# A load stage written as one pinned list of pieces, with a narrower first transform and the weight replicas on another queue

## The chip, the core and the metric

The kernel runs on one core of a Trainium2 chip: TensorE (PE, with its weight loads shown as PEld), VectorE (DVE), ScalarE (ACT), GpSimd (POOL) and SyncE (SP), which share the core's DMA engines. The metric is the device time of one execution in microseconds (us); smaller is better.

## The reference

Two blocks follow each other on x, 4 batches of 32 images (tokens) of 128x128, float32. The first block is what this change touches:

```python
x = x + _L0_conv_ref(_ln_c(x), ...)      # spectral attention over the 32 tokens, then two spectral mixers
t = t + _L0_ffn_ref(_ln_t(t), ...)       # recurrent layer along the rows
x = x + _L1_conv_ref(_ln_c(x), ...)      # 2x up, leaky ReLU, 2x down with given 12x12 filters
t = t + _L1_ffn_ref(_ln_t(t), ...)
```

`_ln_c` normalises every row of 128 values. In `_L0_conv_ref` each token is normalised as an image; keys, queries and values come from a few low frequencies of its Fourier transform times learnt weights, plus a skip; a softmax over 32x32 token pairs per head mixes the values; the result is projected, added to the tokens, and goes through two mixers that again multiply low frequencies. The kernel uses that most of this is linear: it needs of each image only its low-frequency spectrum and the products of images with each other (a Gram matrix), and mixes whole images by one 128x128 matrix (CTbd).

## The kernel before, in words

**Load stage (up to the first channel mix).** XA holds all images with the row index h on the partitions. SP loads them in 16 DMAs of 512 KB (`load`), with constants and small weights between them. Work is in eight half batches k of 16 images. For each: `stats` takes the row statistics on DVE and their inverse root (ACT's Sqrt and a Newton step on DVE); `normalise` scales each image in place, on ACT or DVE by the image's number; `transform` multiplies each image (as the 128x128 stationary operand) with a table of 130 columns (L862): 64 for the low-frequency spectrum and 66 for a real basis of the Gram product. ACT copies three images at a time out of PSUM (L863). A second transform gives the spectrum (ps_pf, L870) and the Gram operand (ps_pr, L874, copied to Rn by L879). Then SP writes the normalised half batch to DRAM (`normed`, L881).

Per batch, `scores` turns the spectrum: ACT copies it from PSUM (L888) and DVE transposes 32x32 blocks (L889). It is spread to all heads (ps_fr, Frep), multiplied on DVE with replicated key/query weights (L909, L923, L924) and brought by PE transposes to the scores psc. `gram` forms the image products pg. `attend` is the softmax and ends in a block of CTbd (L1020). `weights` prepares the learnt weights: Mx (key/query) and Dx (value/projection) go to DRAM and come back replicated to all partitions (`everywhere`, five DMAs each on SP, tiles md and dd, into Mrep and Drep); the first mixer's weights go through DRAM as m1d, transposed, and come back to every partition (L723, L724). `filters` checks that the given filters are of rank one and makes their taps (tile hankel).

After the last normed write SP reloads all images in the other layout, channels on the partitions (L1071, XR, eight DMAs of 1 MB). Each waits for the writes of `normed` and for the readers of XA.

**After it.** The next stage interleaves the channel mix (pm, L1092, with CTbd and XR) with weighted spectra: 32 DVE products `df` (L1286, from Drep and Frep, a ring of eight) and sums on PE (ps_y, L1299, eight steps of four). Then norms, the token-mixing stage (230 to 410 us in the profile), the recurrence, the convolutions and the second recurrence.

**What sets the order.** Inside `with in_order():` each instruction of PE, DVE, ACT and POOL is chained to the one before it on its engine, so the order of the program text is kept. In the load stage the text is generated by Python generators stepped in turns (`step`), and the middle part is outside any `in_order`, so the framework's scheduler places it. The later stages are strings of piece names (SUMS, NORMS, MIXERS, CONVOLUTIONS), walked in order. SP is not chained.

Of the kernel before, what the change touches and what calls it, by code (L numbers as in the profile page):

```python
# [32 lines left out]
P = 128  # L33
NB, NT = 4, 32
NH = 16
# [119 lines left out]
    IRI0.2 M4b.1 de.1 M4c.1 FHG.1 gBc.1 g3.2 Z0.2 FS2.0 Z1.2 g2.2 QG0.1 FS1.0 FS0.0 g1.2 g0.2 ST2.2 A2.2 sq2.2 FS3.0  # L155
    IRS0.1 TA1.1 ZS2.2 AF.0 sq3.2 ST0.2 QG1.1 PW.0 ZS3.2 ZD.2 A0.2 TA0.1 PF.2 sq0.2 R1a.1 sq1.2 LD2.1 FZ.2 SQ.2
    R0b.1 R0a.1 FHIa.3 R1b.1 AO.0 IRS2.1 M1.2 TA2.1 LD0.2 FHIb.3 R2b.1 XN1a.0 XN0b.0 PS.2 M2.2 TA3.1 QI0.3 XN0a.0
    PG1.2 XN1b.0 QI1.3 R2a.1 PG2.2 XT0.0 M2b.2 IRI2.3 R3a.1 R3b.1 XC0.0 XT1.0 P2.2 IRI0.3 Z2.3 M3.2 Z3.3 WX0.0 XC1.0
    P3.2 XN2a.0 al.2 Z0.3 M4a.2 g2.3 M4b.2 g3.3 Z1.3 g0.3 de.2 GB.2 M4c.2 BN0.0 g1.3 FS2.1 FS1.1 ZS2.3 ST2.3 sq1.3
    sq2.3 FHG.2 ST0.3 QG0.2 XN3b.0 IRS0.2 A2.3 A0.3 TA1.2 gBc.2 TA0.2 XN2b.0 FS3.1 PF.3 sq0.3 FS0.1 WC0.0 XT2.0  # L160
    ZS3.3 QG1.2 sq3.3 WX1.0 FZ.3 ZD.3 R1b.2 AF.1 R0b.2 IRS2.2 SQ.3 TA3.2 XC2.0 PW.1 R0a.2 PG1.3 R1a.2 M1.3 BN1.0
    LD2.2 PS.3 TA2.2 R3a.2 XN3a.0 WC1.0 M2.3 AO.1 WX2.0 R2a.2 FHIa.4 BN2.0 R3b.2 PG2.3 XN0b.1 FHIb.4 M2b.3 XT3.0
    P2.3 XN0a.1 M3.3 WC2.0 al.3 QI0.4 R2b.2 QI1.4 P3.3 XC3.0 IRI0.4 XN1a.1 XT0.1 Z1.4 M4a.3 IRI2.4 WX3.0 XN1b.1 Z0.4
    XC0.1 g1.4 M4b.3 de.3 g0.4 M4c.3 Z3.4 Z2.4 GB.3 FHG.3 BN3.0 FS3.2 g3.4 FS1.2 FS2.2 LD0.3 QG0.3 ST0.4 g2.4 FS0.2
    gBc.3 A0.4 QG1.3 ZS3.4 ZS2.4 IRS0.3 sq1.4 TA1.3 sq2.4 ST2.4 LD2.3 R1a.3 TA0.3 A2.4 WC3.0 PF.4 R1b.3 XN2b.1 FZ.4
    AF.2 ZD.4 XT1.1 sq3.4 R0b.3 WX0.1 IRS2.3 PW.2 R0a.3 SQ.4 sq0.4 PG1.4 TA2.3 XC1.1 M1.4 PS.4 BN0.1 TA3.3 AO.2 M2.4
    M2b.4 R2b.3 XN3a.1 XN2a.1 WC0.1 XT2.1 FHIa.5 R3b.3 LD0.4 R3a.3 XC2.1 P2.4 XN3b.1 XN0b.2 M3.4 PG2.4 XN0a.2 P3.4
    FHIb.5 QI0.5 QI1.5 XT3.1 WX1.1 IRI0.5 al.4 R2a.3 XN1a.2 XC3.1 BN1.1 M4a.4 Z1.5 IRI2.5 de.4 WC1.1 M4b.4 M4c.4
    XN1b.2 FS0.3 GB.4 gBc.4 WX2.1 XT0.2 BN2.1 g1.5 XN2b.2 Z3.5 WC2.1 FHG.4 FS3.3 XC0.2 QG0.4 WX3.1 FS1.3 FS2.3 QG1.4
    LD2.4 XT1.2 XN2a.2 XN3a.2 IRS0.4 XC1.2 TA1.4 BN3.1 Z2.5 TA0.4 AF.3 g2.5 Z0.5 R1b.4 XT2.2 IRS2.4 g0.5 WC3.1  # L170
    FHIa.6 sq0.5 R1a.4 R0a.4 R0b.4 WX0.2 ZS2.5 PW.3 g3.5 ZS3.5 BN0.2 TA2.4 AO.3 FHIb.6 ZD.5 ST2.5 sq2.5 FS0.4 R2b.4
    XN3b.2 ST0.5 XC2.2 sq1.5 R2a.4 sq3.5 WC0.2 A0.5 TA3.4 WX1.2 R3b.4 BN1.2 A2.5 PF.5 QI0.6 IRI0.6 XN0a.3 R3a.4
    XN0b.3 XT3.2 Z0.6 WC1.2 FZ.5 SQ.5 M1.5 QI1.6 PG1.5 XC3.2 g0.6 Z1.6 IRI2.6 PS.5 Z2.6 M2.5 g1.6 WX2.2 Z3.6 g2.6
    g3.6 P2.5 BN2.2 M2b.5 M3.5 XN1a.3 XT0.3 FS2.4 PG2.5 P3.5 FS3.4 XC0.3 ST0.6 al.5 M4a.5 WC2.2 A0.6 ST2.6 de.5
    M4b.5 M4c.5 WX0.3 A2.6 BN0.3 XN1b.3 PF.6 ZS2.6 sq0.6 ZS3.6 sq3.6 FS1.4 GB.5 FZ.6 FHG.5 WC0.3 SQ.6 QG0.5 WX3.2
    sq2.6 AF.4 IRS0.5 TA0.5 PW.4 PG1.6 sq1.6 gBc.5 XT1.3 QG1.5 M1.6 XC1.3 LD0.5 ZD.6 BN3.2 TA1.5 R0a.5 XN2a.3 R0b.5
    PS.6 LD2.5 AO.4 IRS2.5 M2.6 XN3b.3 XN2b.3 TA3.5 WC3.2 XT2.3 P2.6 M2b.6 XN3a.3 WX1.3 XC2.3 R1a.5 PG2.6 XT3.3
    TA2.5 R1b.5 FHIa.7 FHIb.7 XN0a.4 R3a.5 BN1.3 M3.6 R2a.5 XN0b.4 XC3.3 WC1.3 WX2.3 XN1b.4 QI0.7 R2b.5 XT0.4 P3.6
    QI1.7 R3b.5 al.6 BN2.3 M4a.6 de.6 XN1a.4 IRI0.7 IRI2.7 XN2b.4 XC0.4 WC2.3 Z1.7 LD0.6 M4b.6 WX3.3 g1.7 XT1.4
    M4c.6 BN3.3 FHG.6 XC1.4 WC3.3 WX0.4 Z0.7 Z2.7 FS2.5 g0.7 FS0.5 g2.7 GB.6 Z3.7 FS1.5 QG0.6 ST0.7 g3.7 BN0.4  # L180
    IRS0.6 FS3.5 A0.7 sq0.7 ZS2.7 TA1.6 ST2.7 gBc.6 ZS3.7 XN2a.4 ZD.7 WC0.4 QG1.6 A2.7 TA0.6 XT2.4 PF.7 R1b.6 sq1.7
    R1a.6 sq3.7 LD2.6 WX1.4 AF.5 FZ.7 R0a.6 SQ.7 XN3b.4 IRS2.6 PW.5 R0b.6 PG1.7 sq2.7 TA2.6 M1.7 LD0.7 XC2.4 PS.7
    AO.5 XN0a.5 XN3a.4 BN1.4 WC1.4 XN0b.5 R2a.6 M2.7 R2b.6 TA3.6 XT3.4 XN1a.5 XC3.4 WX2.4 R3b.6 M2b.7 P2.7 PG2.7
    XN1b.5 BN2.4 WC2.4 XT0.5 M3.7 WX3.4 R3a.6 al.7 P3.7 BN3.4 M4a.7 de.7 XC0.5 LD2.7 FS2.6 M4b.7 XT1.5 XN2b.5 XC1.5
    GB.7 WC3.4 M4c.7 FS3.6 XN2a.5 gBc.7 WX1.5 BN1.5 WC1.5 FS0.6 XT2.5 FHG.7 WX0.5 QG0.7 FS1.6 XN3b.5 AF.6 BN0.5
    IRS0.7 WC0.5 TA0.7 R0a.7 QG1.7 XC2.5 TA1.7 PW.6 XN3a.5 TBL.7 WX2.5 XT3.5 IRS2.7 R1a.7 AO.6 BN2.5 XN0b.6 TA2.7
    XC3.5 XN0a.6 R0b.7 WC2.5 R1b.7 XN1b.6 XT0.6 XN1a.6 XC0.6 FS1.7 FS0.7 WX3.5 AF0.7 XT1.6 BN3.5 TA3.7 XN2b.6 R2a.7
    R2b.7 XN3b.6 WC3.5 WX0.6 XN2a.6 XC1.6 XN3a.6 XT2.6 WX1.6 XC2.6 BN0.6 PW0.7 XT3.6 FS2.7 AO0.7 WC0.6 R3b.7 R3a.7
    WX2.6 BN1.6 XN02a.7 XN00a.7 FS3.7 XN00b.7 XC3.6 XN02b.7 WC1.6 WX3.6 XT02.7 XT00.7 XC02.7 XC00.7 AF2.7 WX02.7
    BN2.6 BN3.6 WC2.6 WC3.6 PW2.7 AO2.7 XN20b.7 WX00.7 XN22b.7 XN20a.7 XN22a.7 XT20.7 BN02.7 BN00.7 XC20.7 XT22.7  # L190
    XC22.7 WX20.7 BN20.7 WC00.7 WC02.7 WX22.7 BN22.7 WC20.7 WC22.7
# [15 lines left out]
C_E = 0  # L207

C_DW = C_E + 130
C_CR = C_DW + 96  # L210
C_SW = C_CR + 128
C_EH2 = C_SW + 256
# [10 lines left out]
C_N = C_DB + NB  # L223
# [8 lines left out]
def _constants():  # L232
    c = np.zeros((P, C_N), np.float64)
# [14 lines left out]
    basis = np.concatenate([(h2[:, None] % 2 == np.arange(2)) / np.sqrt(32), np.cos(turn) / np.sqrt(32),  # L248
                            np.sin(turn) / np.sqrt(32)], 1)
    c[:, C_E + 64 : C_E + 128] = rows.real.T @ basis  # L250
    c[:, C_E + 128 : C_E + 130] = (rows.imag.T @ basis)[:, :2]
# [3 lines left out]
    c[:, C_CR : C_CR + 64] = cols.real  # L255
    c[:, C_CR + 64 : C_CR + 128] = -cols.imag
# [10 lines left out]
    for b in range(NB):  # L267
        o = 32 * b
        c[o : o + KW, C_SW : C_SW + 128] = sw.real
        c[o : o + KW, C_SW + 128 : C_SW + 256] = sw.imag  # L270
        c[o, C_DCB + o : C_DCB + o + 32] = 1.0


        c[o + 1 : o + 9, C_CL : C_CL + 16] = 128.0
        c[o, C_CL : C_CL + 8] = 128.0

        c[o, C_SIG] = -1.0
        c[o : o + 32, C_DB + b] = 1.0
        c[o, C_DCM] = 1.0
        c[o : o + 32, C_ID : C_ID + 32] = np.eye(32)  # L280
        c[o : o + 32, C_BO + o : C_BO + o + 32] = 1.0
        c[o : o + KW, C_TP] = twice[:, 0]
    return np.ascontiguousarray(c.astype(np.float32))
# [3 lines left out]
def _network(  # L287
# [94 lines left out]
    def row_stats(st, n, mean, var):  # L382

        d = sm([P, NG], "rw_d")[:, :n]
        tt(mean, st[:, :, 1], st[:, :, 4], ALU.add)
        ts(mean, mean, 0.5, None, ALU.mult)
        tt(d, st[:, :, 1], st[:, :, 4], ALU.subtract)
        stt(d, d, 0.25, d, ALU.mult, ALU.mult)
        tt(var, st[:, :, 2], st[:, :, 5], ALU.add)
        stt(var, var, 1.0 / P, d, ALU.mult, ALU.add)  # L390
# [170 lines left out]
    ndcm = aw.tile([P, 1], F32, name="ndcm")  # L561
# [28 lines left out]
    nc.sync.dma_start(cst[:, :C_SW], consts[:, :C_SW])  # L590

    for v in range(4):
        nc.gpsimd.dma_start(skips[:, v : v + 1], scal[v * NH : v * NH + NH].unsqueeze(0).broadcast_to([8, NH]))
    load(0, 2 * TC)
    load(0, 3 * TC)
    taps_in = []
    if redo is not None:
        for k in range(2):
            F = wp.tile([2 * PAD + 1, 2, 12], F32, name=f"F{k}")
            taps_in.append(F)  # L600
            for j in range(2):
                f = up[j, 0] if k == 0 else dn[j]
                nc.gpsimd.dma_start(F[:, j, :], f[P // 2 - PAD : P // 2 + PAD + 1, :, P // 2])
    nc.sync.dma_start(cst[:, C_SW:], consts[:, C_SW:])
    for b in range(1, NB - 1):
        for t0 in range(0, NT, TC):
            load(b, t0)
    nc.gpsimd.memset(CTbd, 0.0)
    nc.gpsimd.tensor_copy(rep4, cst[:, C_ID : C_ID + 32].unsqueeze(1).broadcast_to([P, 4, 32]))

    dram = early.enter_context(tc.tile_pool(name="replicas", bufs=1, space=bass.MemoryType.DRAM))

    def weights():

        mw_, mp_ = skips[:, 2:3], skips[:, 3:4]

        def hermitian(wr, wi, d, dm):

            tt(d, wr[:, 31:0:-1], wr[:, 1:], ALU.subtract)
            ts(d, d, dm, 0.5, ALU.mult, ALU.mult)
            tt(wr[:, 1:], wr[:, 1:], d, ALU.add)
            tt(d, wi[:, 31:0:-1], wi[:, 1:], ALU.add)
            ts(d, d, dm, -0.5, ALU.mult, ALU.mult)
# [1791 lines left out]
```

## Time and profile before

| | |
|---|---|
| three runs | 869.56, 870.73, 875.28 us; median 870.73 |
| profiled execution | 870.38 us, span 868.6 us |
| mean granted PE clock | 0.939 |
| busy over the span | PE 750.8, DVE 710.9, ACT 649.4, POOL 361.2 us |
| DMA | 83.22 MB; HBM read 47.46 MB, written 33.66 MB |
| first statistics / first normalisation | 6.38 / 17.67 us |
| last normed write issued / first reload issued | 106.4 / 111.6 us |
| first channel mix / first ps_y | 136.83 / 141.60 us |

A group's row gives line, engine, operation, output and inputs, shape and count, then busy time and mean duration. A row of the timeline gives start and length of a run of equal instructions, and in brackets the idle time before it and what ended it. A stage's row gives its length and each engine's busy time with the count of instructions, the granted PE clock, the mean busy share of the DMA engines, and GB/s.

### The profile page before, as it was taken

The page shows a single profiled execution, that of the slowest core. Times are in us where ns is not written, and L with a number is a line of the kernel's source. Part 1 is how long each engine was busy: PE and PEld are TensorE (multiplying, and loading weights), DVE is VectorE, ACT ScalarE, POOL GpSimd, SP SyncE. Part 2 cuts the span into 40 slices and gives each one's busy share as a digit, 9 for nine tenths or more (in the row PEclk, how much of TensorE's full clock was granted, in tenths as well). Part 3 has the DMA queues.
Part 4 walks back from the last instruction along what each step waited for, and adds up shares of the span by engine and source line. Part 5 has one row for each costly group of instructions (what it writes and reads, how often), then busy time and mean ns, then how long its engine had stood idle before and what let it go on. Part 6 is the DMA issues. An engine that isn't in the chain of part 4 may idle for free.

```text
span 868.6 us, 31057 instructions
## 1 busy us (share of the span) xinstructions
PE 750.8 (86%) x12550; PEld 560.5 (65%) x12550; DVE 710.9 (82%) x2330; ACT 649.4 (75%) x1669; POOL 361.2 (42%) x604
## 2 busy tenths in 40 slices
PE   1799967977878999899779979999999999998994
PEld 1566633336645555645349968888788877875994
DVE  3789668976598899899889978977878877677996
ACT  2588934585738689989779977887777887776994
POOL 2000000011435444365310016788788786961263
PEclk9799967996789899999999969999999999999998
DMA  9954992349611011120000000111111111118454
GB/s 224 260 153 94 250 366 103 137 204 276 162 51 49 26 49 35 42 73 25 25 1 1 1 3 17 40 41 40 28 41 28 41 28 40 40 40 291 172 186 148
DMA packets 105130, 83.22 MB, mean 96 GB/s; under 512 B 5457, under 2 KB 98129, under 8 KB 102865
## 3 DMA queue, kind: packets, MB, share of 16 engines
q1 hardware_dynamic: 104641, 80.86, 31.2%
q8 instruction: 101, 1.65, 0.8%
q0 software_dynamic: 288, 0.01, 0.2%
q14 instruction: 52, 0.43, 0.2%
q10 hardware_dynamic: 48, 0.26, 0.1%
HBM read 47.46 MB, written 33.66 MB: 93 GB/s over the span
## 4 chain that ended last, share of the span: by engine, by line
PE 44%; DVE 25%; ACT 14%; POOL 9%; issue 5%; DMA 1%; SPq 1%; DVEq 0%; ACTq 0%; POOLq 0%
PE ps_k L2068 5%; PE ps_scan L1915 4%; DVE XA L1587 4%; PE ps_d L2198 4%; ACT WXY L1917 4%; DVE XA L1586 4%; PE ps_st L862 3%; ACT yw L1917 3%; POOL XN L2047 3%; PE pm L1092 3%; PE ps_st L1429 3%; PE ps_r L2068 2%; PE ps_e L2205 2%; PE ps_y L1299 2%; POOL xn L2047 2%
## 5 line engine op out<-in xcount | busy, mean ns | idle before, releaser
L2188 DVE SCALAR_TENSOR_TENSOR U<-raw 128x512 f32<-128x512 f32 x128 | 89.8, 731 | 27.8 <-ACT raw L2180 27.6
L1916 DVE SCALAR_TENSOR_TENSOR ps_scan<-WXY,bs,ps_scan 128x128 f32<-128x128 f32 x376 | 105.5, 352 | 1.8 <-PE ps_scan L1915 0.8
L2068 PE MATMUL ps_k<-WXY,q 64*64 64x134 f32 x2048 | 86.0, 282 | 0.9 <-ACT WXY L2152 0.3
L2180 ACT COPY raw<-ps_k 128x512 f32<-128x512 f32 x128 | 71.0, 597 | 17.0 <-PE ps_k L2068 14.6
L2198 PEld LDWEIGHTS ps_d<-WXY,U 128*64 128x64 f32 x2048 | 66.7, 137 | 19.5 <-issue 12.1
L2047 POOL TENSOR_SCALAR XN<-XA,c_r,c_o 128x128 f32<-128x128 f32 x120 | 74.7, 631 | 5.0 <-issue 2.2
L2047 POOL TENSOR_SCALAR xn<-XA,f_r,f_o 128x128 f32<-128x128 f32 x120 | 67.2, 569 | 18.1 <-PE ps_x L2068 12.1
L2198 PE MATMUL ps_d<-WXY,U 128*64 128x67 f32 x2048 | 73.4, 224 | 1.2 <-ACT q L2211 0.9
L2068 PEld LDWEIGHTS ps_k<-WXY,q 64*64 64x64 f32 x2048 | 60.7, 135 | 6.4 <-DVE U L2188 0.8
L862 PE MATMUL ps_st<-cst,XA 128*128 128x130 f32 x256 | 42.8, 313 | 24.9 <-ACT XA L845 22.1
L2068 PE MATMUL ps_r<-WXY,XN 64*64 64x134 f32 x1024 | 59.0, 290 | 2.8 <-DVE XN L2047 1.3
L862 PEld LDWEIGHTS ps_st<-cst,XA 128*128 128x128 f32 x256 | 35.9, 212 | 29.1 <-ACT XA L845 23.1
L1644 ACT ACTIVATE xn<-XA,f_o,f_r 128x128 f32<-128x128 f32 x120 | 51.0, 489 | 4.6 <-DVE f_o L1626 3.4
L1423 ACT ACTIVATE Z<-Z,k,aB 128x128 f32<-128x128 f32 x128 | 51.0, 480 | 4.2 <-DVE Z L1418 4.0
L1586 DVE SCALAR_TENSOR_TENSOR XA<-ps_inv,r1B,xin 128x128 f32<-128x128 f32 x128 | 44.1, 345 | 8.1 <-PE ps_inv L1579 8.1
L1587 DVE SCALAR_TENSOR_TENSOR XA<-Z,gB,XA 128x128 f32<-128x128 f32 x128 | 46.3, 362 | 5.0
L2166 ACT COPY q<-ps_r 128x512 f32<-128x512 f32 x64 | 38.2, 597 | 13.2 <-PE ps_r L2068 12.8
L2027 POOL TENSOR_TENSOR c_r<-c_e,neg_half 128x16 f32<-128x16 f32 (+2 forms) x10 | 25.6, 2563 | 53.3 <-DVE c_e L2020 53.1
L506 PE MATMUL ps_inv<-invq,cst 64*128 64x512 f32 x128 | 41.4, 674 | 3.9 <-ACT invq L497 3.2
L456 PE MATMUL ps_wx<-xt,wvt 128*128 128x512 f32 x64 | 35.9, 643 | 6.7 <-ACT WXY L463 5.5
L845 ACT ACTIVATE XA<-XA,p_n,p_r 128x128 f32<-128x128 f32 x80 | 35.4, 491 | 7.6 <-DVE p_n L829 7.6
L2205 PE MATMUL ps_e<-WXY,q 128*64 128x67 f32 x1024 | 40.8, 222 | 0.0
(441 smaller groups left out, 2100.8 us busy)
## 6 DMA issues: line engine op xcount, KB each, us to landing
XA<-in_x_dram SPq DMA_DIRECT2D x16, 512.0 KB, 7.2
normed<-XA SPq DMA_DIRECT2D x8, 1024.0 KB, 6.1
XA<-normed SPq DMA_DIRECT2D x8, 1024.0 KB, 10.4
mixed<-XA SPq DMA_DIRECT2D x8, 1024.0 KB, 3.8
XA<-mixed SPq DMA_DIRECT2D x32, 256.0 KB, 5.3
xin<-in_x_dram SPq DMA_DIRECT2D x32, 256.0 KB, 3.3
turned<-XA SPq DMA_DIRECT2D x32, 256.0 KB, 2.5
out_dram<-res SPq DMA_DIRECT2D x52, 128.0 KB, 2.1
```

The source lines that it names most:

```text
L862: mm(p[:, i, :], XA[:, b, t0 + j + i, :], cst[:, C_E : C_E + 130], start=True, stop=True)
L1423: nc.scalar.activation(z, z, AF.Gelu, bias=k1, scale=aB[:, j : j + 1])
L1586: stt(a, p2[c, b][:, i], r1B[:, j : j + 1], xin[c, b - b % 2][:, b % 2, i], ALU.mult, ALU.add)
L1587: stt(a, Z[c][:, b, i], gB[c][:, n : n + 1], a, ALU.mult, ALU.add)
L1916: stt(p4, WX[:, :, h, :], s[:, 0:1], p4, ALU.mult, ALU.add)
L1917: nc.scalar.activation(dst, p4, AF.Sigmoid, bias=s[:, 1:2])
L2047: e.tensor_scalar(dst, src_, r, o, ALU.mult, ALU.add)
L2068: m = mm(dst, data, taps, start=(n == 0 and (i, j) not in last), stop=(n == 1), skip_group_check=True)
L2180: nc.scalar.copy(raw[u, k], banks["k", u][:, k])
L2188: stt(U[u][:, k].rearrange("p k s m -> p (k s m)"), v, SLOPE, v, ALU.mult, ALU.max)
L2198: mm(p[HALVES[s], m, b, REACH[k]], U[v][:, b, k, s, HALVES[m]], DR[:, k, REACH[k]], start=(m == 0 and b == 0 and k == 0), stop=(k == 1), s ...
L2205: mm(p[HALVES[j], b * P : b * P + P][:, REACH[m]], q3[v - 1][:, m, b, HALVES[j]], DC[:, m, REACH[m]], start=(b == 0 and m == 0), stop=(m = ...
```

## The change

1. **The load stage becomes a list.** LOADING is a string of some 600 pieces (S statistics, VA/VQ/VB/VC their factors, N and Nv normalisation on ACT or DVE, T, A, F, R, C the transforms and their copies, W the normed write, E to p the scores, G, g, H the Gram product, a, x, P, n, c the softmax, s scales, w weights). It is walked inside one `in_order` that also chains SP. The eight reloads of XR follow in the same block. Statistics are grouped as half batches 0, 1, 2+3, 4+5, 6+7; 90 images are normalised on ACT and 38 on DVE (80 and 48 before).
2. **First transform to 65 columns.** One real basis of 65 columns serves both the spectrum and the Gram operand; signs and scales move into second-transform tables. ACT or DVE copies seven, six and three images at a time.
3. **The spectrum is turned from PSUM**: the DVE transpose reads ps_pf with a stride; ACT's copy goes.
4. **Replicas by GpSimd's queue.** `everywhere` and the loads of value weights, vectors, mixer weights, ffn weights and filter taps, and the zeroing of hankel, are issued by POOL. Image loads, normed writes, m1d with its read-back, and the reloads stay on SP. All 16 image loads are issued before anything else of SP but the tables and constants.
5. **Weight symmetrisation** takes two ACT scalings and two DVE operations in place of six DVE operations. The scalar `ndcm` becomes a constant column.
6. **The filter check leaves the load stage**: it runs as nine pieces FL in MIXERS (token mixing).

```diff
+    first[:, C_F : C_F + 64] = rows.real.T @ basis
+    first[:, C_F + 64] = rows.imag.T @ basis[:, 0] / np.sqrt(2)
...
-    nc.sync.dma_start(cst[:, :C_SW], consts[:, :C_SW])
+    nc.sync.dma_start(tables, consts[:, C_N:])
...
+    for b in range(1, NB):
+        for t0 in range(0, NT, TC):
+            load(b, t0)
+        if b == 1:
+            nc.sync.dma_start(cst, consts[:, :C_N])
...
+    def T(k, i):
+        b, t0 = tokens(k)
+        j, n = next((j, i0) for j, (i0, i1) in enumerate(IMAGES) if i < i1)
+        if i == n:
+            held["st1", k, j] = psa.tile([P, 7, 65], F32, tag="st1", name="ps_st1")
+        mm(held["st1", k, j][:, i - n, :], XA[:, b, t0 + i, :], tables[:, C_F : C_F + 65], start=True, stop=True)
...
+    def W_(k, i):
+        b, t0 = tokens(k)
+        nc.sync.dma_start(normed[HB * k : HB * k + HB].rearrange("n h w -> h n w"), XA[:, b, t0 : t0 + HB, :])
+
+    def E_(b, i):
+        held["F4", b] = sp.tile([P, 16, NT], F32, tag="F4", name="F4")
+        nc.vector.transpose(held["F4", b].rearrange("p k w -> p (k w)"), held.pop(("pf", b)).rearrange("p t k -> p k t"))
...
+    def everywhere(t, dst, name):
+        n = t.shape[1]
+        d = dram.tile([NH, 8, n], F32, name=name)
+        nc.gpsimd.dma_start(d.rearrange("h k n -> k h n"), t)
+        for h in range(4):
+            nc.gpsimd.dma_start(dst[32 * h : 32 * h + 32],
+                                d[h::4].rearrange("g k n -> g (k n)").unsqueeze(0).broadcast_to([32, 4, 8 * n]))
+
+    def hermitian(w, d):
+        for r in range(2):
+            nc.scalar.mul(d[:, r], w[r][:, 31:0:-1], half_dc[: d.shape[0]])
+
+    def hermitian_sum(w, d):
+        for r in range(2):
+            stt(w[r][:, 1:], w[r][:, 1:], rest_dc[: d.shape[0]], d[:, r], ALU.mult, (ALU.add, ALU.subtract)[r])
...
+        elif k == 4:
+            everywhere(Mx.rearrange("p a w -> p (a w)"), Mrep.rearrange("p g k r m -> p g (k r m)"), "md")
+            nc.gpsimd.dma_start(Wv.rearrange("p w r k -> p (w r k)"), spec[:, W_VA:W_M1])
+            nc.gpsimd.dma_start(sc, scal.partition_broadcast(P))
...
+        elif k == 9:
+            held["mirv"] = big("ps_mirv")
+            mirrors(held["mirv"], Wv[:, 1], 4)
...
+        elif k == 13:
+            everywhere(Dx.rearrange("p a w -> p (a w)"), Drep.rearrange("p g k r j w -> p g (k r j w)"), "dd")
...
+        elif k == 16:
+            d = dram.tile([2 * KH, KW], F32, name="m1d")
+            nc.sync.dma_start(d.rearrange("k w -> w k"), m12[:KW, 0].rearrange("p r k -> p (r k)"))
+            nc.sync.dma_start(m1T.rearrange("p r k w -> p (r k w)"),
+                                d.rearrange("k w -> (k w)").unsqueeze(0).broadcast_to([P, KW * 2 * KH]))
...
+    with in_order(mybir.EngineType.SP):
+        for piece in LOADING.split():
+            name = piece.rstrip("0123456789.")
+            k, _, i = piece[len(name) :].partition(".")
+            loading[name](int(k), int(i or 0))
+        for h in range(0, P, ROWS):
+            nc.sync.dma_start(XR[:, h : h + ROWS, :], normed[:, h : h + ROWS, :])
+    early.close()
...
+        filtering = filters(m1, lambda name: psf.tile([P, 512], F32, tag="t", name=name))
+
+        def FL(c, k):
+            next(filtering)
```

The end of the list, from the last normalisation (N7.10) on:

```diff
+    T7.7 q2 qc2 a1.3 a1.4 T7.8 T7.9 T7.13 T7.11 N7.10 K2.5 T7.12 C5 T7.15 T7.14 T7.10 F6 A7.1 A7.2 W4 t2.0 F7 w14.0
+    t2.2 x1 w14.1 w15.0 tc2.0 tc2.2 t2.1 tc2.1 E3 r3.0 w13 rc3.0 r3.2 r3.3 rc3.3 a1.5 a1.6 a1.7 r3.1 rv3.2 W5 P1 G2
+    W6 a1.8 rc3.1 FK3 K3.0 K3.1 K3.2 g2 R6 H2 C6 W7 n0 a2.0 R7 C7 K3.3 p2 a2.1 q3 qc3 G3 g3 K3.4 w16 a2.2 K3.5 t3.0
+    H3 a2.3 a2.4 tc3.0 x2 w15.1 t3.2 t3.1 a2.5 a2.6 tc3.2 a2.7 P2 w17 a3.0 a2.8 tc3.1 p3 a3.1 a3.2 c1 a1.9 a3.3 a3.4
+    x3 c0 a3.5 a3.6 a3.7 P3 a0.9 a3.8 n3 n2 c2 a2.9 c3 a3.9 n1
```

## The prediction, before the changed kernel was run

> **What bounds it now.** I read the stages first, cut where the first channel mix starts (136.8 us) and where the token-mixing stage begins.
>
> ```profile
> core 0: us, PE busy (x) PEld busy (x) DVE busy (x) ACT busy (x) POOL busy (x), PEclk, DMA share, GB/s
> 0.00:20.00 20.00, 1.78 (x8) 1.79 (x9) 6.92 (x38) 3.22 (x7) 6.27 (x18) 1.00 0.95 219
> 20.00:110.00 90.00, 77.20 (x810) 56.93 (x810) 71.93 (x323) 71.07 (x177) 0.68 (x3) 0.94 0.79 193
> 110.00:136.80 26.80, 14.93 (x170) 8.71 (x162) 16.69 (x72) 6.94 (x16) 1.46 (x2) 0.63 0.81 325
> ...
> 230.00:410.00 180.00, 158.36 (x1615) 96.28 (x1615) 159.86 (x561) 140.71 (x389) 84.10 (x200) 0.95 0.15 42
> ```
>
> Up to 136.8 us DVE works 6.92 + 71.93 + 16.69 = 95.5 us, PE 93.9, ACT 81.2. No engine fills the stage: DVE idles 41 us. The last 27 us are a tail in which PE's clock falls to 0.63. The chain of waits shows what the tail is: one dependent sequence, with little beside it.
>
> ```profile
> 121.53 1.43 DVE KM L909 x2
> ...
> 129.57 0.20 DVE sums L772
> ...
> 136.83 4.84 PE pm L1092 x6
> 141.67 2.11 PE ps_y L1299 x32
> ```
>
> The fourth batch's scores, the filter check (L772) and its softmax run one after the other; the stage after it then starts on DVE (df, 1.29 us each) and PE at once. The reload of the normalised images was long under way. At the other end of the stage one row of the timeline matters: DVE sits 4.82 us on the constants, for a scalar that nothing early needs, with the statistics' last steps behind it.
>
> ```profile
> 17.07 0.15 DVE L717 TENSOR_SCALAR ndcm<-cst 128x1 f32<-128x1 f32 x1 [4.82 <-DMA cst<-in_consts_dram]
> ```
>
> **The change by parts.**
>
> *First transform, 130 to 65 columns.* I take nothing for PE. Rows of equal tile and unequal width:
>
> ```profile
> 102.32 0.83 PE L862 MATMUL ps_st<-cst,XA 128*128 128x130 f32 x6
> ...
> 346.68 3.79 PE L1429 MATMUL ps_st<-cst,Z 128*128 128x64 f32 x32
> ```
>
> One matmul of either takes 0.275 us, so the spacing is (0.83 - 0.275)/5 = 111 ns at 130 columns and (3.79 - 0.275)/31 = 113 ns at 64: the load of 128x128 weights sets it. The Trainium skill (TensorE: Matmul & The Clock Gate, Back-to-back issue gap) gives N/2.4 + 2.5 ns for an isolated matmul, which would save 256 x 65/2.4 = 6.9 us; the same section warns that in pairs with weight loads this under-counts. The rows decide: 0. What the narrow result does save is its eviction on ACT, and the spectrum's extra copy:
>
> ```profile
> L863 ACT COPY A<-ps_st 128x390 f32<-128x390 f32 (+1 forms) x48 | 21.0, 447 | 9.7 <-PE ps_st L862 9.0
> ...
> L888 ACT COPY FF<-ps_pf 128x512 f32<-128x512 f32 x4 | 4.2, 1040 | 3.2 <-PE ps_pf L870 3.2
> ```
>
> 24 copies of 455, 390 and 195 columns, by the trace's 0.26 us at 130 and 0.48 at 390, cost 8 x (0.54 + 0.48 + 0.32) = 10.7 us: minus 10.3. The FF copy goes: minus 4.2. Back come ten normalisations at 0.39 us spacing (plus 3.9) and the two scalings of the weights (about plus 1). ACT: 81 to about 71 us. The transpose that reads PSUM with a stride is in no row: between 0.71 us (L889 from SBUF) and 1.04 (ACT reading the same layout), so 0 to 1.3 us for four; I take 0, the same engine's row.
>
> *DVE.* The filter check leaves this stage (two filters of about 3.8 us, 7.5 in all), ten normalisations (0.25 us spacing, 2.5) and three of six weight operations leave (2.2); three evictions come (1.1). 95.5 becomes 84 us. DVE stays the busiest engine.
>
> *The pinned order.* The wait on the constants goes (4.8 us), and the softmaxes and scores of all batches are laid between other pieces. The nearest row for what a piecewise written order attains is the token-mixing stage, 230 to 410 us: DVE busy 159.9 of 180, 89%. With the first statistics at 6.4 us, DVE ends at 6.4 + 84/0.89 = 101 us, plus some 4 us of round trips in the last softmax (132.18 to 136.83 is 4.6 us for 2.9 us of DVE work): about 105, not 136.8. At 80% (the present 72 of 90) it would be 115.
>
> *The reload behind the mixer's weights.* This takes the place of the removed wait, I think. SP is now pinned too, and in its order the write of the eighth half batch is followed by the first mixer's weights turned through DRAM (m1d, its read-back), then by the eight reloads. SP's queue before:
>
> ```profile
> 68.87 0.89 SPq L723 DMA_DIRECT2D m1d<-m  x1
> 69.86 11.76 SPq L748 DMA_DIRECT2D hankel<-fzero  x1
> ...
> 111.64 5.06 SPq L1071 DMA_DIRECT2D XA<-normed  x8
> ```
>
> The write of m1d is 1,088 packets of 4 bytes; they occupy the queue from 70.9 to 82.7 us, 11.8 us at nearly 0 GB/s, and the next issue stands for all of it. Today that lies where DMA has nothing else to do. Afterwards its read-back must wait on SP for the landing, with all eight reloads queued behind it. The sum: DVE work after the last normalisation in the list is 26 softmax pieces (7.7), 7 products (4.7) and small ones (3.6), 16 us; so the normalisations end at 6.4 + 68/0.89 = 83. Write of 1 MB, issue to landing 5.2 us in this trace (106.43 to 111.64), and some 4 more because the value replicas (2.2 MB, 11 us in this trace) now fall beside it: 92. m1d 11.8: 104. Landing noticed and read-back issued: 106. Its 0.55 MB (2 us) and the first reload (7.7, the shortest of the eight in the trace): 116. Three mixes at 0.5: ps_y can start at 117.5, against 141.6. If nothing but DVE counted, ps_y would start a df group of 4.8 us after 105, at 110. So 24 us are gained, not 32. DVE runs two df groups ahead meanwhile; then PE's 4.95 us per step (2.84 + 2.11) sets the pace as it does now.
>
> *Replicas on POOL's queue.* The copies of the weights to all partitions leave SP; POOL issues 17 DMAs in a row after the query/key product (Mx, 25.1 us in the trace less most of the 4.8 us wait: about 22): md and its four reads, the value weights, vectors, mixer weights, fw, zeros, taps. Behind them on POOL stands nothing urgent. Who waits is PE, in its order, at the value weights' mirrors, and DVE at the key products: the pieces listed ahead of them hold 28 and 39 us of DVE work, so at 6.4 + 28/0.89 = 38 and 50 us.
>
> ```profile
> 2.56 1.84 POOL L593 DMA_DIRECT2D skips<-in_scal_dram  x3
> 4.35 1.22 POOL L603 DMA_DIRECT2D F<-in_up_dram  x2
> ```
>
> By these rows one issue costs 0.6 us, also with 84 elements in it. md lands at most 5.4 us after its issue (25.75 to the reads at 31.2). Value weights issued: 22 + 5.4 + 6 x 0.65 = 31.3, landed 5 us later, 36: in time. Against this stands the Trainium skill (SBUF — State Buffer, SBUF: two separate sides, the box on DVE blocking software-generated DMA): POOL can't write descriptors while DVE runs a two-port operation, and a DMA of 0.62 us took 3.1. Then the weights land at 22 + 5.4 + 18.6 + 5 = 51, 13 us late, and PE passes that on. The only POOL DMA here with DVE busy beside it, the taps at 132.5 us, took 0.56; it lies among tiny operations, but I take 0.65 and keep 13 us for the range.
>
> *Filter check moved.* Nine pieces, 7.5 us of DVE, into 250 to 330 us, where DVE is 85 to 95% busy and carries most of the chain: 0 if they fall into its gaps, 8 if not; I take 4, as that stage is bound by DVE about half of the time. Its PE products are eight tiny ones.
>
> **Sum.** The profiled execution took 870.4 us (span 868.6 and 1.8 around), the median 870.7. 870.4 - 24 + 4 = 850.
>
> **Rivals.**
> (a) The m1d write is hidden or quick, DVE alone sets the end: 870.4 - 32 + 4 = 842. For it: four bytes were slow in a queue already full. Against: 0 GB/s for ten of those microseconds.
> (b) The order wastes what it frees: another 80% or less of DVE. 84/0.75 gives DVE's end at 118 and 122 with the tail, ps_y at 127; and the normalisations move to 97, ps_y by the reload to 131. Gain 10, minus 4: 864.
> (c) Slower: POOL's descriptors starve and PE stands at the value weights. It decides from the point where 24 - 4 = 20 us are lost, the weights landing at 58, that is 4.2 us for each of six issues; at 6 us each they land at 68, and the time is 880. For it the skill's box and DVE at over 80%; against it the rows of 0.6.
> (d) The narrow transform brings PE nothing: built into all cases.
>
> **Chances.** Forecast 0.60 (844 to 858), (a) 0.20 (836 to 846), (b) 0.12 (856 to 870), (c) 0.08 (860 to 895). Under 1% (8.7 us) this kernel can't be told from no change; faster by over 1% means below 862: 0.60 + 0.20 + 0.05 of (b), 0.85. Within 1%: the other 0.07 of (b) and 0.02 of (c), 0.09; slower 0.06. Eight in ten: 837 to 863.
>
> **What would show it.** First normalisation near 13 us, not 17.7. L862's successor still spaced 111 ns. The last normalisation near 83 us; an SP issue of m1d after the last normed write, a read-back some 12 to 15 us later, then the eight reloads; the first mix waiting for a DMA and not for DVE. If the first mix follows the last CTbd addition at once, (a) or (b) holds. If PE stands near 40 us on the value weights, (c). If 230 to 410 us grows by more than 8 us, the filter pieces were mispriced. The forecast fails if the normalisations end well after 90 us.

## The result, and the profile after

The changed kernel takes 898.32 us (median of four, 895.63 to 899.48), the kernel before 870.14 beside it: the ratio is 1.031, with a 95% interval of 1.026 to 1.0361. The forecast was 850 us. The profiled execution took 899.48 us, with a span of 897.7 us (868.6 before). Executions over 1.5% above the fastest of the same kernel are left out of the medians and ratios below: three of twenty of e7_three_mended, one of four of e10_wider.

Where the 29 us came from is read from a few points that both programs pass:

| us from the start | before | after | later by |
|---|---|---|---|
| last normed write issued (SP) | 106.43 | 116.57 | 10.1 |
| first channel mix (pm, PE) | 136.83 | 152.85 | 16.0 |
| first ps_y (PE) | 141.60 | 157.45 | 15.9 |
| first FuT (norms) | 182.54 | 198.00 | 15.5 |
| first ps_scan (end of token mixing) | 448.97 | 477.11 | 28.1 |
| end | 868.6 | 897.7 | 29.1 |

So the load stage lost 16 us, in place of the 24 it was to gain, and the stretch from the first FuT to ps_scan, which no part of the change but the filter pieces touches, grew from 266.4 to 279.1 us. Everything else kept its length to within 1 us.

The stage view of the changed kernel, 40 to 100 us (length, then busy time and count of PE, PEld, DVE, ACT and POOL, the granted PE clock, DMA share, GB/s):

```profile
40.00:60.00 20.00, 20.00 (x137) 15.29 (x137) 9.96 (x46) 9.93 (x26) 2.04 (x6) 0.50 0.86 240
60.00:80.00 20.00, 20.00 (x152) 13.30 (x151) 7.51 (x32) 9.28 (x24) 0.00 (x0) 0.50 0.12 32
80.00:100.00 20.00, 20.00 (x116) 17.44 (x119) 8.99 (x25) 10.72 (x26) 0.00 (x0) 0.50 0.24 69
```

The same rows of the kernel before:

```profile
40.00:60.00 20.00, 17.71 (x188) 11.90 (x187) 18.55 (x79) 17.26 (x42) 0.68 (x3) 1.00 0.78 200
60.00:80.00 20.00, 17.73 (x225) 13.13 (x223) 18.60 (x85) 17.33 (x48) 0.00 (x0) 1.00 0.26 58
80.00:100.00 20.00, 17.98 (x156) 12.82 (x157) 17.27 (x74) 17.30 (x42) 0.00 (x0) 1.00 0.91 218
```

In the changed kernel PE is busy without a gap, at half its clock, and DVE works 26.5 of 60 us, where it worked 54.4: it waits. The clock record of the trace says it exactly: 0.5 from 37.1 to 105.4 us, where the kernel before had 1.0 from 38.5 to 117.0. PE has become the engine that bounds the load stage.

The timeline of the changed kernel (start, length, engine, line, operation, tiles, shape, count; in brackets the idle time before it and what ended it):

```profile
12.66 1.65 ACT L728 ACTIVATE XA<-XA,p_n,p_r 128x128 f32<-128x128 f32 x4 [1.16 <-DVE p_n L708]
...
26.79 2.23 POOL L959 DMA_DIRECT2D WXY<-md  x4 [5.15 <-DMA md<-Mx]
29.01 0.52 POOL L1008 DMA_DIRECT2D WXY<-in_spec_dram  x1
...
38.82 1.01 PE L946 MATMUL ps_mirv<-ident,WXY 1*128 1x1 f32 x8 [4.22 <-DMA WXY<-in_spec_dram]
39.76 3.25 PE L737 MATMUL ps_st<-tables,XA 128*128 128x65 f32 x14
...
116.57 0.36 SPq L772 DMA_DIRECT2D normed<-XA  x1
119.84 0.30 SPq L1053 DMA_DIRECT2D m1d<-m  x1
145.47 0.35 SPq L1054 DMA_DIRECT2D WXY<-m1d  x1
146.06 4.37 SPq L1077 DMA_DIRECT2D XA<-normed  x8
...
152.85 4.68 PE L1091 MATMUL pm<-XA,WXY 128*128 128x512 f32 x6 [15.56 <-DMA XA<-normed]
```

Four things are seen. The first normalisation is at 12.66 us: the wait on the constants is gone. PE stands 4.22 us for the value weights. The transform's records follow each other, at this clock, by (3.25 - 0.42)/13 = 0.218 us, twice the 111 ns of before (0.42 is the length of one). And SP's order is the one foreseen, m1d's write, read-back, eight reloads, with the first mix waiting for a reload; but from the write to the read-back it takes 25.6 us.

### The profile page after: what moved, and what is told of

Its sections match the earlier page's. It is cut to its first block, busy times and chain, and to the rows that moved or that the text cites. A ratio compares the mean times of both kernels' runs of the same rounds, so it can differ in the third digit from the quotient of the medians.

```text
span 897.7 us, 31035 instructions
## 1 busy us (share of the span) xinstructions
PE 777.2 (87%) x12566; PEld 580.0 (65%) x12566; DVE 706.4 (79%) x2310; ACT 642.3 (72%) x1654; POOL 372.6 (42%) x622
## 5 line engine op out<-in xcount | busy, mean ns | idle before, releaser
L1981 DVE SCALAR_TENSOR_TENSOR ps_scan<-WXY,bs,ps_scan 128x128 f32<-128x128 f32 x376 | 105.5, 351 | 1.9 <-PE ps_scan L1980 1.1
L737 PE MATMUL ps_st<-tables,XA 128*128 128x65 f32 x256 | 53.2, 371 | 8.1 <-ACT XA L728 7.8
L737 PEld LDWEIGHTS ps_st<-tables,XA 128*128 128x128 f32 x256 | 48.0, 278 | 17.3 <-ACT XA L728 8.2
L1285 DVE TENSOR_TENSOR df<-WXY 128x1088 f32<-128x1088 f32 x32 | 38.8, 1285 | 15.8 <-PE ps_y L1298 15.8
L1091 PE MATMUL pm<-XA,WXY 128*128 128x512 f32 x64 | 32.1, 642 | 16.2 <-DMA XA<-normed 15.6
L499 PE MATMUL ps_wx<-xt,wvt 128*128 128x512 f32 x64 | 38.5, 686 | 6.3 <-ACT WXY L506 5.3
```

The costliest lines, as they stand in the source:

```text
L737: mm(held["st1", k, j][:, i - n, :], XA[:, b, t0 + i, :], tables[:, C_F : C_F + 65], start=True, stop=True)
L1981: stt(p4, WX[:, :, h, :], s[:, 0:1], p4, ALU.mult, ALU.add)
```

## Experiments

Times are medians, and ratios are against the kernel before, run beside each, with 95% intervals. Points inside a run (a write, the first ps_y, the clock) are those of its one profiled execution.

### What holds the clock at half

Three theories went into the first runs: (A) the narrow matmuls, (B) PE's stand for the value weights, (C) the pinned order as such.

```diff
 # e1_wide, in T
+        out, w = held["st1", k, j], tables[:, C_F : C_F + 65]
+        if i == 6:
+            held["six", k] = True
+        if j == 0 and ("six", k) in held:
+            mm(out[:, i, :], XA[:, b, t0 + i, :], w, start=True, stop=True)
+        else:
+            o = i - n
+            mm(out[:, o : 7 : 6 - o, :], XA[:, b, t0 + i, :], w.unsqueeze(1).broadcast_to([P, 2, 65]),
+               start=True, stop=True)
```

> The changed kernel, with the moving side of most first-transform matmuls (about 13 of every 16) 130 columns wide again: the same 65 columns streamed twice, the second time into a PSUM row that nobody reads. Instructions, order and results are the same. Theory A (65 columns between weight loads give the array too little to do, and the clock is granted at half): the granted clock is back at 1.0 from about 42 us to beyond 90 us, the last normed write is issued near 90 us instead of 116.6, and the time falls by 15 to 27 us, to 871 to 883 us. Theory B (PE's 4.2 us stand for the value weights trips the clock, and the width has no part in it): clock 0.5 from 37 to 105 us as before, and a time of 897 to 901 us, the wider stream costing a little more. Theory C (the pinned order itself keeps PE waiting): PE not busy all the time, the time within 3 us of 898.

Measured: 888.39 us, ratio 1.0175 (1.0109 to 1.0241), some 10 us less than the changed kernel. The stage view of this run:

```profile
40.00:60.00 20.00, 20.00 (x135) 14.85 (x135) 10.04 (x46) 9.41 (x24) 1.77 (x5) 0.50 0.84 237
60.00:80.00 20.00, 20.00 (x200) 15.57 (x200) 11.32 (x45) 14.21 (x38) 0.00 (x0) 0.88 0.12 33
80.00:100.00 20.00, 20.00 (x212) 15.50 (x211) 17.99 (x62) 17.29 (x41) 1.01 (x2) 1.00 0.58 162
```

With twice the columns to stream, the same list runs faster: the clock is back at 1.0 from 61.5 us on, but for 3.4 us, and the last normed write goes out at 99.4 instead of 116.6. That is theory A's direction, and less than it said: the clock was to be back at 42 us, and the time to be 871 to 883.

```diff
 # e2_values: out of piece w4, into a piece w18 behind w0.1
-            nc.gpsimd.dma_start(Wv.rearrange("p w r k -> p (w r k)"), spec[:, W_VA:W_M1])
...
+        elif k == 18:
+            nc.gpsimd.dma_start(Wv.rearrange("p w r k -> p (w r k)"), spec[:, W_VA:W_M1])
...
-w0.1 w1.1
+w0.1 w18 w1.1
```

> The changed kernel, with the load of the value and projection weights issued on GpSimd's queue right after the first weights have been read (piece w0.1) instead of behind the replicas' reads, so that PE does not stand for them at 34.6 us. Theory B: no stand, so the clock stays at 1.0 behind 37 us, the last normed write comes near 90 us, and the time falls by 15 to 27 us. Theory A: the stand is gone, but the clock falls to 0.5 within some 10 us all the same, and the time falls by no more than the stand, 0 to 5 us: 893 to 898 us.

Measured: 894.08 us, ratio 1.0258 (1.0181 to 1.0335). PE stands nowhere between 30 and 60 us, and yet the clock falls at 46.1 us, for 54.6 us; the last normed write is at 111.8. Theory B is refuted. Even the 4 us are not clearly the stand's. The run on the filter copy below has the changed kernel's load stage unaltered; in its profile PE came to the mirrors at 39.25 us, just late enough not to wait, its clock fell at 46.1 us too, and its last normed write also went out at 111.8.

```diff
 # e4_narrow_alone, in the kernel before
-                    mm(p[:, i, :], XA[:, b, t0 + j + i, :], cst[:, C_E : C_E + 130], start=True, stop=True)
-                nc.scalar.copy(A1[:, j : j + m, :], p[:, :m])
+                    mm(p[:, i, :65], XA[:, b, t0 + j + i, :], cst[:, C_E : C_E + 65], start=True, stop=True)
+                nc.scalar.copy(A1[:, j : j + m, :].rearrange("p m (a c) -> p m a c", a=2),
+                               p[:, :m, :65].unsqueeze(2).broadcast_to([P, m, 2, 65]))
```

> The kernel before, in its own order, with one part of the change alone: the first transform's matmuls have 65 moving columns instead of 130 (the other columns of the transform are left out: the copy from PSUM, as long as before, reads the 65 twice). Theory A: the granted clock, 1.0 from 38.5 to 117 us in the kernel before, is at 0.5 for most of that stretch, PE is busy nearly all of it, and the time grows by 8 to 25 us, to 878 to 895 us. Theories B and C (the stand, or the new order): the clock stays at 1.0, and the time is within 4 us of the kernel before, 866 to 874 us.

Measured: 889.19 us, ratio 1.0187 (1.012 to 1.0255). Its stage view:

```profile
40.00:60.00 20.00, 18.44 (x150) 14.01 (x153) 16.36 (x72) 13.34 (x33) 0.58 (x3) 0.78 0.58 146
60.00:80.00 20.00, 19.09 (x148) 12.92 (x148) 12.58 (x63) 13.54 (x33) 0.00 (x0) 0.71 0.20 54
80.00:100.00 20.00, 18.14 (x192) 13.01 (x190) 15.29 (x70) 14.52 (x38) 0.00 (x0) 0.83 0.63 131
```

In the old order, with no stand and half of the transform left out, the clock is at 0.71 and 0.83 from 60 to 100 us where it was 1.00, the first mix comes at 157.6 instead of 136.8 us, and the kernel is slower by 1.9%. The 0.78 of the first row is too high: this trace's clock record begins at 47.9 us, and ahead of its first entry the views print 1.00. PE's timeline has there

```profile
37.60 5.96 PE L862 MATMUL ps_st<-cst,XA 128*128 128x65 f32 x27
```

which is a record every (5.96 - 0.42)/26 = 0.213 us, the half clock. With that stretch counted the clock is at half for 48 of the 78.5 us from 38.5 to 117, most of it, as theory A said; the new list, denser in the same narrow matmuls, keeps it there for 68 us on end. Nothing but the width was changed (the copy out of PSUM kept its length, 0.486 us against 0.483). That shows the cause, against B and C: narrow columns alone cost the clock. All profiles of this case agree: from 38 us to the last normalisation the clock is at half for at least 37 us in each of the nine with 65 columns (in e11_no_dd by the spacing of the records), and for 0.5 to 31 us in the four with 130 (the kernel before, e1_wide, e8_three_mended_wide, e10_wider).

### The round trip of m1 in front of the reloads

```diff
 # e5_reload_first: w16 leaves its place in LOADING
         for h in range(0, P, ROWS):
             nc.sync.dma_start(XR[:, h : h + ROWS, :], normed[:, h : h + ROWS, :])
+        w_(16, 0)
```

> The changed kernel, with the write of m1 and its read-back as 128 replicas (piece w16) moved on SyncE's queue behind the eight reloads, so that the reloads wait for the last normed write alone. m1's replicas are first needed in the spectral normalisation, tens of us later. Theory (the reloads stood behind the 25.6 us round trip of m1): they go out near 121 us, have landed when the last CTbd block is done at 137.4 us, the first mix starts at about 138 us instead of 152.9, ps_y at 142 to 145 instead of 157.5, and the time falls by 12 to 15 us, to 883 to 886 us. Rival (the eight-fold replicas on GpSimd's queue, or m1's own 4-byte packets, hold the reloads up as well): the first mix not before 148 us, and the time 893 to 899 us.

Measured: 883.27 us, ratio 1.0121 (1.0048 to 1.0194). The timeline of this run:

```profile
110.34 0.36 SPq L772 DMA_DIRECT2D normed<-XA  x1
117.24 4.85 SPq L1077 DMA_DIRECT2D XA<-normed  x8
131.59 0.29 SPq L1053 DMA_DIRECT2D m1d<-m  x1
160.38 0.34 SPq L1054 DMA_DIRECT2D WXY<-m1d  x1
...
131.70 5.30 PE L1092 MATMUL pm<-XA,WXY 128*128 128x512 f32 x6 [0.29 <-DVE WXY L877]
```

The first mix now follows the last CTbd block by 0.29 us and waits for no transfer; m1's trip takes 28.8 us and nobody waits for it. The reloads did stand behind it, as forecast. Not all of the 21 us by which the first mix is earlier is this edit's: the last normed write, ahead of it in the order, went out 6 us earlier too. But why 25.6 us and not the forecast's 14?

```diff
 # e9_m1_before_dd, in LOADING
-w15.0 tc2.0
+w15.0 w16 tc2.0
...
-K3.4 w16 a2.2
+K3.4 a2.2
```

> The changed kernel, with m1's round trip (w16) moved forward on SyncE's queue, directly behind the piece that makes m1 (w15.0) and so ahead of the replicas of dd on GpSimd's queue and of the last three normed writes. Theory (the 4-byte packets of m1 were slow because the replicas of dd, in 4,352-byte packets on another queue, went ahead of them on the DMA engines): from write to read-back 15 to 18 us (15.7 in the kernel before, 25.6 in the changed one), the reloads go out behind the last normed write near 120 us, the first mix starts at 133 to 138 us, and the time is 881 to 888 us. Rival (the trip is slow for its own 1,088 elements, in that stage or in any): 23 us or more, the last normed writes stand behind it, and the time is 889 to 899 us.

Measured: 902.91 us, ratio 1.0353 (1.0293 to 1.0413). The edit missed its aim: DVE came to w15.0 only at 117.7 us, when GpSimd had already issued the reads of dd. Write to read-back took 22.3 us, between the two forecasts; the time lies above both. The last three normed writes stood behind it on SP, as the rival had said of its own case:

```profile
117.67 0.30 SPq L1053 DMA_DIRECT2D m1d<-m  x1
140.02 0.35 SPq L1054 DMA_DIRECT2D WXY<-m1d  x1
140.46 7.68 SPq L772 DMA_DIRECT2D normed<-XA  x3
153.85 4.07 SPq L1077 DMA_DIRECT2D XA<-normed  x8
```

So the dispute was put by itself, with dd's round trip taken out:

```diff
 # e11_no_dd, piece w13
-            everywhere(Dx.rearrange("p a w -> p (a w)"), Drep.rearrange("p g k r j w -> p g (k r j w)"), "dd")
+            nc.gpsimd.memset(WXY[:, 0:4352], 0.0)
```

> The changed kernel without the round trip of dd through DRAM: GpSimd clears Drep instead, so the value product is left out of the result (the products with it are still made). Theory (m1's packets stood behind the 2.2 MB of dd's replicas): from m1's write to its read-back 15 to 17 us instead of 25.6, the reloads 8 to 11 us earlier, the first mix at 138 to 146 us (no earlier than the last CTbd block, about 134 to 138), and the time 884 to 891 us. Rival (pinned SyncE, or the landing of the last normed write beside m1's, makes the trip long): 22 us or more with no replicas beside it, and the time 894 to 899 us.

Measured: 883.23 us, ratio 1.0115 (1.0064 to 1.0165). The timeline of this run:

```profile
120.01 0.30 SPq L1053 DMA_DIRECT2D m1d<-m  x1
134.53 0.35 SPq L1054 DMA_DIRECT2D WXY<-m1d  x1
135.12 4.29 SPq L1077 DMA_DIRECT2D XA<-normed  x8
...
142.39 4.82 PE L1091 MATMUL pm<-XA,WXY 128*128 128x512 f32 x6 [4.88 <-DMA XA<-normed]
```

The write of m1 goes out within 0.2 us of the changed kernel's (120.01 against 119.84), and then the trip takes 14.5 us. The other 11.1 were dd's replicas. The DMA view of the changed kernel shows how, first from 121 to 132 us, then from 132 to 144 (packets, and for each queue packets, MB and the share of the 16 engines):

```profile
DMA packets 882, 2.37 MB, mean 216 GB/s; under 512 B 86, under 2 KB 374, under 8 KB 880
...
q0 software_dynamic: 557, 2.20, 94.5%
...
DMA packets 1090, 0.05 MB, mean 4 GB/s; under 512 B 1083, under 2 KB 1083, under 8 KB 1089
...
q1 hardware_dynamic: 1070, 0.00, 11.0%
```

While GpSimd's queue q0 moves the replicas, hardly a small packet passes; when it is through, 1,070 of m1's 1,088 go out in the next 12 us.

### The filter pieces in the mixing stage

VectorE's wait at the copy of the filter's sums, in the changed kernel (durations ns min/median/max, first and last start; idle before it):

```profile
L1352 DVE COPY sums<-ps_f x2: 184/185/186, 273.5 to 313.2; 7x38 f32<-7x38 f32 x2
...
  PE ps_f L1350: 10.6, 2
```

Two copies of 0.19 us, and 10.6 us of waiting for two pairs of tiny matmuls. DVE's instructions, paired one by one with those of the kernel before, are 15.7 us late until the first filter's pieces, 19 to 20 behind its copy, and some 28 behind the second's.

```diff
 # e3_filter_copy
-            sums = small_([n, 24 + 2 * n], "sums")
-            nc.vector.tensor_copy(sums, p[:n, : 24 + 2 * n])
             yield True
+            sums = small_([n, 24 + 2 * n], "sums")
+            nc.vector.tensor_copy(sums, p[:n, : 24 + 2 * n])
...
-gBc.2 TA0.2
+gBc.2 FL.0 TA0.2
...
-R2a.2 FL.0 FHIa.4
+R2a.2 FHIa.4
```

> The changed kernel, with the filter pieces cut elsewhere: the copy of the sums out of PSUM goes one piece later than the two matmuls that make them (for the second filter the matmuls go forward behind gBc.2 and the copy takes their old place). Nine pieces and the same instructions. Theory: VectorE waited in its pinned place for sums that PE, with other work queued ahead, came to 3.2 and 7.4 us later; with the gap the waits are gone, the stretch from 222 to 477 us of the changed kernel gets shorter by 8 to 12 us, and the time is 886 to 890 us. Rival (the pieces' own instructions, or the PSUM bank that they borrow, cost it): the stretch keeps its 255 us to within 3, and the time is 895 to 899 us.

Measured: 890.71 us, ratio 1.021 (1.0134 to 1.0286). The stretch from FuT to ps_scan is 274.1 us, 5 less and not 8 to 12. The same row of this run says why:

```profile
L1353 DVE COPY sums<-ps_f x2: 178/182/186, 272.2 to 303.5; 7x38 f32<-7x38 f32 x2
...
  PE ps_f L1350: 5.2, 1
```

The first filter's wait is gone, the second's is still 5.2 us. Half a success: it shows that the place in the order made the wait, not that one piece's distance is enough to end it.

```diff
 # e6_filters_back: nine pieces fl0 in LOADING for the nine FL.0 in MIXERS
-        filtering = filters(m1, lambda name: psf.tile([P, 512], F32, tag="t", name=name))
+    filtering = filters(wp, big) if redo is not None else None
+
+    def fl(k, i):
+        if filtering is not None:
+            next(filtering)
```

> The changed kernel, with the nine filter pieces taken out of the mixing stage's order and put back into the load stage (every fifteenth to twentieth piece from the 300th on, the two matmuls one piece ahead of the copy of their sums). Theory: in the mixing stage they cost 12.5 us (3.3 at the first filter's sums, 8 at the second's): the stretch from the first FuT to ps_scan, 279.1 us in the changed kernel and 266.4 in the kernel before, goes back to 265 to 268 us, the load stage, where VectorE waits for TensorE anyway, grows by 0 to 4 us, and the time is 884 to 890 us. Rival (the stretch is longer for another reason, such as the phase of the clock): it stays above 275 us, and the time is 895 to 901 us.

Measured: 882.85 us, ratio 1.0111 (1.0034 to 1.0188). The stretch is 264.5 us, and the load stage did not grow (ps_y at 156.4, against 157.5). The filter pieces cost some 279.1 - 264.5 = 14.6 us where the change had put them, and nothing that can be told from that stage's spread of 6 us (last section) where they had been.

### Together

The edits of e2, e5 and e6 in one kernel, with the narrow transform:

> The changed kernel with three things mended and the narrow transform kept: value weights loaded early, m1's round trip behind the reloads, filter pieces back in the load stage. Theory (the three costs are apart from each other, and narrow columns go on holding the clock at half): last normed write near 112 us, first mix near 132, ps_y 136 to 140 us, and a time of 863 to 872 us, within 1% of the kernel before. Rival (one of the mended waits hid another that takes its place): 875 to 890 us.

Measured: 869.86 us, ratio 0.9959 (0.9934 to 0.9984): within half a per cent of the kernel before. ps_y came at 130.9 us, earlier than expected, with the clock at half for 37.6 us of 48.5 to 93; but the profiled execution, 862.22 us, was the fastest of the twenty. Then with the wide edit of e1 on top:

> The same three mended, and most first-transform matmuls 130 columns wide as in the run before on width. Theory: the clock at 1.0 through most of 40 to 95 us, last normed write near 95 us, first mix near 118 to 122 us, ps_y 123 to 128 us (141.6 in the kernel before), and a time of 848 to 857 us. Rival (the load stage's end is then set by the replicas' DMAs or by VectorE's order): ps_y not before 135 us, and 860 to 868 us.

Measured: 858.98 us, ratio 0.981 (0.9721 to 0.9898), just outside what was expected. ps_y at 129.0; but the clock was at half from 39.7 to 60.2 and from 70.4 to 80.7 us. Whether the narrow matmuls that are left held it there, the next run tests by making 15 of every 16 wide:

```diff
 # e10_wider, in T
+        if i != 6:
+            o = i - n
+            mm(out[:, o : 7 : 6 - o, :], XA[:, b, t0 + i, :], w.unsqueeze(1).broadcast_to([P, 2, 65]),
+               start=True, stop=True)
+        if j == 0 and len(done) == 7:
+            mm(out[:, 6, :], XA[:, b, t0 + 6, :], w, start=True, stop=True)
```

> The three mended, with 15 of every 16 first-transform matmuls 130 columns wide (the seventh of a group moved behind the other six, so that they can write into its PSUM row first). Theory (the width of this matmul decides the clock by itself): the 20.5 us at 0.5 from 39.7 us and the 10.2 us from 70.4 us, left with 13 of 16 wide, shrink to 10 us or less together, and the time falls by 5 to 10 us against that run, to 849 to 854 us. Rival (the rest of that stretch's work, sums over 32 rows and products of 32 columns, holds the clock as well): 0.5 for 20 us or more of 39 to 81 us again, and a time of 856 to 863 us.

Measured: 851.47 us, ratio 0.9792 (0.9714 to 0.9871). The stage view of this run:

```profile
40.00:60.00 20.00, 20.00 (x184) 13.92 (x182) 15.14 (x75) 11.67 (x30) 0.73 (x4) 0.74 1.11 294
60.00:80.00 20.00, 18.59 (x222) 14.55 (x221) 17.78 (x70) 15.78 (x41) 0.00 (x0) 1.00 0.26 74
80.00:100.00 20.00, 19.20 (x189) 13.82 (x185) 18.58 (x76) 14.58 (x37) 3.40 (x6) 1.00 0.54 146
```

The clock is at half for 10.2 us (42.1 to 52.4) and at 1.0 for the next 61; DVE, which had waited, is busy at 89 and 93% from 60 to 100 us; last normed write 94.7, first mix 116.4, ps_y 121.2 us. Whether the last 7.5 us against e8 are real the intervals do not say (the ratios differ by 0.2%); that both versions beat the kernel before, by some 2%, they do.

## Why the prediction was wrong

The measured 898 us lies outside every range that the prediction gave, rivals included (836 to 895). Its chain to ps_y was: m1d written when the last normed write has landed, at 92, its trip to 106, reload and three mixes to 117.5 us. The changed kernel has 119.8, 145.5 and 157.45. By its terms:

| term | forecast | measured | error, us |
|---|---|---|---|
| m1d's write issued | 92 | 119.8 | +28 |
| m1d's write to its read-back | 14 | 25.6 | +11.6 |
| read-back to ps_y | 11.5 | 12.0 | +0.5 |
| ps_y to FuT | unchanged (40.9) | 40.5 | -0.4 |
| FuT to ps_scan | +4 | +12.7 | +8.7 |
| ps_scan to the end | unchanged | +1.0 | +1.0 |

The sum is some +49, from 850 to the profiled 899.5. The first term is the normalisations: they were to end at 83 and ended at 116.5, with the last normed write at their heels. The prediction had named that as the sign of its failure. (m1d's write then waited 2.8 us for DVE to finish m1, and not for that write's landing, which it did not need.)

**The failed step is "First transform, 130 to 65 columns. I take nothing for PE."** The reading behind it was right: at full clock 65 columns follow each other no faster than 130 (in e2, fourteen records at a clock of 1.0 took 1.78 us, (1.78 - 0.27)/13 = 0.116 us apart). But a width can cost as well as save, and the cost was never bounded: rival (d), "brings PE nothing", was built into all cases as if zero were the worst. What it cost is the first term: with most of the columns doubled the last normed write went out at 99.4 (e1) and, with the other mends, at 94.7 us (e10), so some 17 to 22 of the 33 us came back. In e10, with no trip of m1 ahead of the reloads, ps_y started at 121.2 us; the prediction had 110 for that case. What makes up the 11 us between them no run apportions.

Why narrow columns cost the clock is an inference from rows of the changed kernel's groups (40 to 60 us, at half clock; mean ns last):

```profile
L764 PE MATMUL ps_pr<-A,tables 128*64 128x512 f32 x2 | 2.0, 1088 | 0.0
...
L764 PE MATMUL ps_pr<-A,tables 128*64 128x32 f32 x2 | 0.4, 278 | 0.0
```

A column streams in about (1,088 - 278)/480 = 1.69 ns; 65 columns fill 110 of the 218 ns from one record to the next, 130 would fill all of it. The wide stream keeps the array streaming all of the time, the narrow one half of it, and both count as busy in the profile. The Trainium skill (TensorE: Matmul & The Clock Gate, What's actually happening) has the full clock granted "After ≥1 busy SHORT window (~3.4µs sustained)". By that and the profile's busy column the clock should have come back one such window after PE's stand, near 42 us; the run kept 0.50 to 105 us at 20.00 busy of 20.00. The measurement decides: the profile's busy time of PE is not what grants the clock. What does, and why 10 us stay at half with nearly all matmuls wide, no run here settles.

**The pinned order at 89% of DVE.** It did not fail on its own account. With the clock mended (e10) DVE runs at 17.78 and 18.58 of 20. DVE's work was as forecast, 95.4 us up to the first mix, of which some 10 are df: 85 against 84. ACT had 74.3 against 71. The FF transpose from PSUM took 0.72 us, as assumed.

**The reload behind m1d.** The mechanism was right (e5), and its error, 11.6 us, is the second by size. 14 us was the price of the trip alone, and e11 measured 14.5. The step added 4 us for dd's replicas to the normed write, which they hardly touched (6.0 us from issue to landing, 5.1 before); they fell on m1d, 11 us of them.

**Replicas on POOL's queue.** Issues took 0.5 to 0.6 us, so the trace's rows were right, and the 3.1 us of the Trainium skill (SBUF — State Buffer, A bandwidth-pool intuition that's wrong) were not seen. DVE was busy beside them, with statistics and twelve normalisations; whether those are two-port operations no run shows. The value weights were issued at 29.0, earlier than the 31.3 of the forecast, but took 9.8 us to land in place of 5: 38.8, not 36. So PE stood near 40 us, which the prediction had named as the sign of rival (c), but not for (c)'s reason, slow issues, and the 4.2 us of standing are not a cost that can be told from chance (e2).

**Filter check moved: 4 us, measured some 13 to 15.** The range, "0 if they fall into its gaps, 8 if not", counted DVE's instructions only. The cost is a wait that the nine pieces add: a PE round trip inside a pinned order, with PE's queue ahead of it. That wait, 10.6 us of the two copies, was not named, though the pieces' "eight tiny" PE products were.

What the three misses share: each edit was priced by its own length, and not by what it does to the engine or queue beside it. dd's replicas were even seen, and laid beside the wrong transfer.

## What to carry to other kernels

Before narrowing a matmul, compare its streaming time with its weight load: where the load sets the pace, as here, fewer columns saved nothing, and they took the granted clock, and with it all of PE's other work, down to half. So time both widths in place. In a pinned order price an inserted piece by its round trips: put the consumer of a PE result where PE will already have been, or put the piece into a stage that waits anyway. And keep a transfer of a thousand tiny packets off the queue of anything urgent, and off the engines when another queue moves large ones.

## What the runs showed of the hardware

- A PE that was busy without a gap from 38.8 to 105.4 us, by the profile, ran all of it at a granted clock of 0.50. Streaming each image's columns twice, 130 in place of 65, made the same list faster by 10 us (e1), and by 11 us with the other three costs mended (e7 to e8).
- Stretches at one clock last multiples of about 3.4 us (3.4, 6.8, 10.2, 13.7), and begin at times that differ between executions. With the same code up to there the last normed write went out at 116.6 (the changed kernel), 111.8 (e3) and 110.3 us (e5), with the clock at half for 67, 56 and 51 us from 38 us on. A difference of 4 us in this stage, as in e2, is therefore not yet an effect.
- A trace's clock record begins with its first entry, and ahead of it the views print 1.00 whatever the clock was. In e11 that entry is at 105.5 us, and the row for 60 to 80 us says 1.00, while the transform's records follow each other by 213 ns, as at 0.5 in the changed kernel. The mean clock over the kernel before, 0.939, is too high by up to 0.012 for the same reason (its record begins at 21.4 us, and the spacing ahead of it is 218 ns). Read the spacing of a known instruction beside the clock.
- 1,088 packets of 4 bytes took 14.5 us from issue to the dependent read-back with the DMA engines nearly free (e11), 25.6 beside 2.2 MB of 4,352-byte packets from another queue (the changed kernel), and 28.8 behind the reloads of their own queue, with those replicas over (e5).
